# Half of a copy out of PSUM replaced by a sum that reads PSUM, in a four-layer graph network

## The chip, the cores and the metric

The kernel runs on one core of one Trainium2 chip. The metric is the time of the whole program on the device in microseconds (us), the median of three runs. The engines are named as in the profile: PE is TensorE (matmuls), PEld its weight loads, DVE is VectorE, ACT is ScalarE, POOL is GpSimd, SP is SyncE, which issues all the transfers here.

## The reference, cut to what matters

Sixty-four graphs of 256 nodes with 128 features each pass through four layers, every one closed by a residual and a layer norm. All of them multiply the node features by 256 x 256 matrices that are the same for all graphs:

```python
# layer 0: five gated steps, both matrices are adj
m  = einsum('nm,bmd->bnd', adj, h)
u3 = h @ u3_w.T + u3_b
z  = sigmoid(concat([m, m]) @ w3_w.T + w3_b + u3)
r  = sigmoid(concat([m, m]) @ w4_w.T + w4_b + u3)
hv = tanh(concat([m, m]) @ w5_w.T + w5_b + (r * h @ u5_w.T + u5_b))
h  = (1 - z) * h + z * hv
# layer 1: softmax over masked edges, split into its diagonal and the rest
# layer 2: attention over the edges, then relu(LN(.)), then (1 + eps) * g + adj @ g, two dense layers
# layer 3: adj @ x, adj @ adj @ x, adj @ adj @ adj @ x, each with its own weights
```

The product of a 256 x 256 matrix with the features of two graphs is what the change touches. It is needed eight times for each pair of graphs: five times in layer 0 and once in each of the others.

## The kernel before, in words

The graphs are worked on in 32 pairs, so that one tile is 128 partitions by 512 columns: two graphs, two blocks of 128 nodes each, 128 features. All data are float32. Many pairs are under way at once, and the order in which each engine meets their operations is worked out before the program is written. The class `Schedule` collects every operation with its readers and writers, its engine or a choice of engines, and an estimated duration. `Schedule.order` then repeatedly takes the operation that can start first by its own estimates, gives it the engine on which it would end first, and emits it. `SPARE` (L49) is a bias in that choice: microseconds added to the end an engine would reach, so that a positive number makes the engine less attractive. Its key `"DVE+"` stands for DVE operations that read two SBUF tensors[...] (`USES`, L45). At run time each engine follows its list strictly in order and waits on semaphores.

The helper `spread7` (L553) computes the product with a 256 x 256 matrix by 7 block products of 128 x 128 in place of 8. Its steps, all in one PSUM bank `t` of 512 columns (four blocks):

- three sums of the input blocks (L572, L573, L574), each on DVE or POOL;
- a first group of four block products (L576 to L579, all issued from L566), one into each block of `t`;
- a copy of all four blocks from `t` to the SBUF tile `o` (L580; the helper `evacuate` issues it from L236 on ACT, or from L237 on DVE);
- a sum of 256 columns (L581): blocks 0 and 1 of `o` plus blocks 2 and 3 of `o`, on DVE or POOL;
- a second group of three products (L582 to L584) that accumulate onto blocks 0, 3 and 1 of `t`. Each of them writes the bank that the copy reads, so none starts before the copy has ended;
- a sum of 128 columns (L585, DVE or POOL), a copy of block 0 (L586, again issued from L236) and a last sum of 256 columns that reads `t` (L587, DVE). Its result is the mT or qT that the following matmuls read.

A case of it is used 234 times: in all five steps of layer 0 from the third pair on (150), and in the other three layers for all but the last four pairs (84). The rest goes through `spread` (L542) with 8 block products.

Around it: L684, L685, L692, L699 and L700 are the 512-column matmuls of layer 0; L688, L694 and L703 its three tanh on ACT; L704, L705 and L707 its updates on DVE. L529 is a blockwise transpose on DVE ahead of a transfer out (L531) and back (L537), which turns a tile. L721 are the products of layers 1 and 2, L791 those of the attention, L827, L828 and L835 those of layer 3. L645 and L653 belong to the row scales, L617 and L622 are two ways (DVE, ACT) of a normalization.

Of the kernel before, what the change touches and what calls it, by code (L numbers as in the profile page):

```python
# [12 lines left out]
P = 128  # L13
# [32 lines left out]

AGAIN = {"DVE": 0.12, "POOL": 0.12}

SPARE = {"DVE": 1.0, "DVE+": 0.0, "POOL": -0.3}  # L49


DUE, LAST_DUE, LAST = 15.0, 12.0, 12
# [6 lines left out]
def mm(cols):  # L59

    return cols * 0.00168 + 0.005
# [40 lines left out]
class Schedule:  # L102
# [29 lines left out]
    def order(self, tiles):  # L132
# [14 lines left out]
        while ready:  # L147
            best = None
            for op in ready:
# [7 lines left out]
                for engine, us, fn in op.ways:  # L157
                    us = us if engine == "PE" else us * MARGIN
                    start = max(op.ready, held, *(engines[e] for e in USES.get(engine, (engine,))))
                    end = start + us + SPARE.get(engine, 0.0)  # L160
                    if way is None or end < way[0]:
# [41 lines left out]
def kernel(ctx: ExitStack, tc: tile.TileContext, x, xT, adj, adjT, mats, cols, rows, out):  # L203
    nc = tc.nc
# [10 lines left out]
    def pe(us, fn, r, w):  # L215
        S.add([("PE", us, fn)], r, w)
# [4 lines left out]
    def dve(us, fn, r, w):  # L221
        S.add([("DVE", us, fn)], r, w)
# [11 lines left out]
    def evacuate(o, i, r, w, us=(0.49, 0.61)):  # L234

        S.add([("ACT", us[0], lambda: nc.scalar.copy(o(), i())),  # L236
               ("DVE", us[1], lambda: nc.vector.tensor_copy(o(), i()))], r, w)  # L237
# [242 lines left out]
    def bank():  # L480

        t = Value("PS", name="ps")
        t.full = True
        return t
# [68 lines left out]
    def spread7(h, right, terms):  # L553

        sv, o, t = Value("A", name="sums"), Value("A", name="mT"), bank()
        p1, p2, p4 = (Part(sv) for _ in range(3))
        blk = lambda v, k: v.at(512)[:, k * P:(k + 1) * P]
        H = lambda b, j: lambda: blk(h, 2 * b + j)  # L560
        B = lambda j, i: lambda: right.ap[:, j, i * P:(i + 1) * P]
        T = lambda k: lambda: terms.ap[:, k, :]
        s3, s1, s2, s4 = (lambda k=k: blk(sv, k) for k in range(4))

        def product(k, left, rt, r, start=False):
            pe(mm(128), lambda: nc.tensor.matmul(blk(t, k), left(), rt(), start=start, stop=True, skip_group_check=True),  # L566
               [*r, right, terms, *[t] * (not start)], [t])

        def sum_(us, us_pool, fn, r, w):
            S.add([("DVE+", us, lambda: fn(nc.vector)), ("POOL", us_pool, lambda: fn(nc.gpsimd))], r, w)  # L570

        sum_(0.335, 0.8, lambda e: e.tensor_sub(sv.at(4, P)[:, 0:2], h.at(4, P)[:, 0::2], h.at(4, P)[:, 2:4]), [h], [p1])  # L572
        sum_(0.2, 0.46, lambda e: e.tensor_sub(s2(), s1(), H(0, 0)()), [h, p1], [p2])  # L573
        sum_(0.2, 0.46, lambda e: e.tensor_add(s4(), s2(), H(0, 1)()), [h, p2], [p4])  # L574

        product(0, H(0, 0), B(0, 0), [h], start=True)  # L576
        product(1, s1, T(0), [p1])
        product(3, s3, T(2), [p1])
        product(2, s2, T(1), [p2])  # L579
        evacuate(lambda: o.at(512), lambda: t.at(512), [t], [o])  # L580
        sum_(0.335, 0.8, lambda e: e.tensor_add(sv.at(4, P)[:, 0:2], o.at(4, P)[:, 0:2], o.at(4, P)[:, 2:4]), [o], [p1])  # L581
        product(0, H(0, 1), B(1, 0), [h])  # L582
        product(3, H(1, 1), T(3), [h])
        product(1, s4, B(1, 1), [p4])  # L584
        sum_(0.2, 0.46, lambda e: e.tensor_add(blk(o, 3), blk(sv, 0), blk(sv, 1)), [p1], [o])  # L585
        evacuate(lambda: blk(o, 0), lambda: blk(t, 0), [t], [o], (0.17, 0.2))  # L586
        dve(0.335, lambda: nc.vector.tensor_add(o.at(4, P)[:, 1:3], t.at(4, P)[:, 1::2],  # L587
                                                blk(sv, 0)[:, None, :].to_broadcast([P, 2, P])), [t, p1], [o])
        return o
# [87 lines left out]
    def layer0(x0, hT):  # L677
        h = x0
        for s in range(STEPS):
            mT = spread7(h, aT, aT7) if s in FAST and FIRST <= S.pair < n_pairs - FINAL else to_sbuf(spread(h, aT), "mT")  # L680
            t = bank()

# [43 lines left out]
    def layer1(x1):  # L726
        qT = spread7(x1, offT, offT7) if S.pair < n_pairs - SEVEN["q1"] else to_sbuf(spread(x1, offT), "qT")
        xb = Value("A", name="xb")
        xd = Value("A", name="xd")
        dc = lambda: dcol.ap[:, None, :, None].to_broadcast([P, 2, 2, D])  # L730

        def scaled():
            for c in range(4):
                nc.scalar.mul(tokens(xd)[:, c, :], tokens(x1)[:, c, :], dcol.ap[:, c % 2:c % 2 + 1])
        S.add([("ACT", 1.26, scaled), ("DVE+", TT, lambda: nc.vector.tensor_mul(xd.at(2, 2, D), x1.at(2, 2, D), dc())),
               ("POOL", 1.27, lambda: nc.gpsimd.tensor_mul(xd.at(2, 2, D), x1.at(2, 2, D), dc()))], [x1, dcol], [xd])
        dT = turn(xd, "dT", "x1")
        dve_or_pool(lambda e: e.tensor_add(tokens(xb), tokens(x1), row("l1_bias", 4)), [x1, rbc], [xb])
        t = seed((0.49, 0.61), tokens, lambda: tokens(xb), [xb, qT, dT])
        scale_norm(products([qT, dT], [lambda: mat("l1w1"), lambda: mat("l1w0")], t), x1)  # L740

    def layer2(x2):
# [44 lines left out]
        for b in range(2):  # L787
            def fn(b=b, t=t):
# [11 lines left out]
               ("DVE+", 0.34, lambda: nc.vector.tensor_scalar(hg.at(512), hg.at(512), 0.0, None, op0=ALU.max))], [hg], [hg])  # L800
        dve_or_pool(lambda e: e.tensor_add(tokens(hb), tokens(hg), row("b2", 4)), [hg, rbc], [hb])
        gT = spread7(hg, ginT, ginT7) if S.pair < n_pairs - SEVEN["g"] else to_sbuf(spread(hg, ginT), "gT")
        t, z = seed((0.49, 0.61), tokens, lambda: row("b1", 4), [rbc, gT]), Value("A", name="z")
        scale_norm(products([gT], [lambda: mat("w1")], t), z)
# [97 lines left out]
```

## Time and profile before

| | before |
|---|---|
| device time, median of 3 (lowest to highest) | 1486.76 us (1484.88 to 1487.45) |
| profiled span, first to last instruction | 1485.2 us |
| PE busy | 1474.5 us, 99% |
| DVE busy | 1234.4 us, 83% |
| ACT busy | 1026.9 us, 69% |
| POOL busy | 829.8 us, 56% |
| mean granted TensorE clock | 0.999 |

A busy share says how much of the span an engine had an instruction running. For PE it needs care: matmuls overlap, and their ends are modelled, so that the share alone does not say whether the array is fed without gaps. A group of instructions in the profile is written as line, engine, operation, output<-inputs, shapes, count, then busy time and mean duration of one in ns, then the idle time of the engine ahead of them and what ended it. Each float32 matmul of the program leaves two records in the trace.

### The profile page before, as it was taken

The numbers are of one execution on the slowest core, as the hardware profiler recorded it, in microseconds if no ns is written. First come the engines' busy times: TensorE is split into PE (matmuls) and PEld (weight loads), VectorE is DVE, ScalarE is ACT, GpSimd is POOL, SyncE is SP. The second block draws the span as 40 slices with busy tenths as digits, with TensorE's granted clock in tenths as the row PEclk, the third lists the DMA queues.
The fourth block names the chain that finished last, engine by engine and source line by source line (L and its number), as shares of the span: only waits on it lengthen the run. The fifth ranks groups of instructions, "written<-read, shape, count | busy, mean of one in ns | idle before, by whom it ended". The sixth has DMA issues, their size and how long they took to land.

```text
span 1485.2 us, 28119 instructions
## 1 busy us (share of the span) xinstructions
PE 1474.5 (99%) x7704; PEld 1062.6 (72%) x7704; DVE 1234.4 (83%) x3083; ACT 1026.9 (69%) x3116; POOL 829.8 (56%) x1307
## 2 busy tenths in 40 slices
PE   9999999999999999999999999999999999999998
PEld 6556666666676677777767777777676776788997
DVE  7767888988999899888888888878888888989872
ACT  3444556667777787876776767676686767878875
POOL 4412434555576776564556556565454746676542
PEclk9999999999999999999999999999999999999999
DMA  8544565777788978776778668777777776667762
GB/s 239 121 85 99 104 131 121 144 148 152 156 156 173 176 167 171 161 160 135 148 148 178 134 134 174 155 158 143 142 166 148 151 153 124 136 136 148 165 123 71
DMA packets 946845, 216.60 MB, mean 146 GB/s; under 512 B 726017, under 2 KB 942209, under 8 KB 946689
## 3 DMA queue, kind: packets, MB, share of 16 engines
q1 hardware_dynamic: 946688, 214.81, 70.7%
q8 instruction: 62, 1.02, 0.3%
q14 instruction: 95, 0.77, 0.2%
HBM read 116.86 MB, written 97.85 MB: 145 GB/s over the span
## 4 chain that ended last, share of the span: by engine, by line
PE 95%; DVE 2%; DMA 1%; ACT 0%; issue 0%; SPq 0%; POOL 0%; POOLq 0%; ACTq 0%; DVEq 0%
PE ps L566 23%; PE ps L699 9%; PE ps L700 9%; PE ps L684 9%; PE ps L685 9%; PE ps L692 9%; PE ps L721 7%; PE ps L835 4%; PE ps L828 4%; PE ps L827 4%; PE ps L791 4%; PE ps L548 2%; PE ps L751 2%; DMA x<-x_in 1%; DMA a<-e 0%; DVE a L529 0%
## 5 line engine op out<-in xcount | busy, mean ns | idle before, releaser
L566 PEld LDWEIGHTS ps<-aT,a 128*128 128x128 f32 x2144 | 291.4, 192 | 83.3 <-issue 76.7
L236 ACT COPY a<-ps 128x128 f32<-128x128 f32 (+2 forms) x553 | 230.4, 433 | 137.8 <-PE ps L566 48.6
L566 PE MATMUL ps<-aT,a 128*128 128x128 f32 x2144 | 315.7, 275 | 0.9 <-DMA a<-e 0.5
L585 POOL TENSOR_TENSOR a<-a 128x128 f32<-128x128 f32 x205 | 103.7, 510 | 150.4 <-DVE a L581 110.6
L688 ACT ACTIVATE a<-ps,bzrh 128x512 f32<-128x512 f32 x160 | 110.0, 688 | 104.4 <-PE ps L685 90.7
L703 ACT ACTIVATE ps<-ps,bzrh 128x512 f32<-128x512 f32 x160 | 106.1, 663 | 105.3 <-PE ps L700 102.3
L699 PE MATMUL ps<-a,w 128*128 128x512 f32 x320 | 163.7, 593 | 0.0
L685 PE MATMUL ps<-a,w 128*128 128x512 f32 x320 | 163.4, 592 | 0.0
L700 PE MATMUL ps<-a,u5h 128*128 128x512 f32 x320 | 163.4, 592 | 0.0
L692 PE MATMUL ps<-a,w 128*128 128x512 f32 x320 | 162.8, 593 | 0.0
L645 ACT ACTIVATE a<-ps 128x128 f32<-128x128 f32 x488 | 128.7, 282 | 45.9 <-PE ps L721 20.9
L529 DVE STREAM_TRANSPOSE a<-a 128x512 f32<-128x512 f32 x215 | 149.7, 700 | 10.9 <-DMA e<-a 2.2
L587 DVE TENSOR_TENSOR a<-ps,a 128x256 f32<-128x256 f32 x234 | 96.5, 416 | 67.8 <-ACT a L236 32.0
L721 PE MATMUL ps<-W,a 128*128 128x128 f32 x1024 | 144.5, 275 | 0.0
L721 PEld LDWEIGHTS ps<-W,a 128*128 128x128 f32 x1024 | 132.8, 192 | 16.1 <-issue 13.9
L653 POOL TENSOR_TENSOR s<-s,neg_half 128x4 f32<-128x4 f32 x128 | 138.1, 1079 | 7.6
L694 ACT ACTIVATE a<-ps,bzrh 128x512 f32<-128x512 f32 x160 | 110.5, 691 | 45.2 <-PE ps L692 37.8
L684 PE MATMUL ps<-a,W 128*128 128x512 f32 x256 | 131.0, 593 | 0.0
L685 PEld LDWEIGHTS ps<-a,w 128*128 128x128 f32 x320 | 60.8, 190 | 76.5 <-issue 68.1
L700 PEld LDWEIGHTS ps<-a,u5h 128*128 128x128 f32 x320 | 60.8, 190 | 76.5 <-issue 64.8
L705 DVE SCALAR_TENSOR_TENSOR ps<-a,ps 128x512 f32<-128x512 f32 x160 | 109.7, 686 | 6.1 <-ACT a L694 4.4
L573 POOL TENSOR_TENSOR a<-a,a 128x128 f32<-128x128 f32 x133 | 67.3, 507 | 83.6 <-DVE a L572 55.3
(208 smaller groups left out, 3329.2 us busy)
## 6 DMA issues: line engine op xcount, KB each, us to landing
e<-a SPq DMA_DIRECT2D x277, 256.0 KB
a<-e SPq DMA_DIRECT2D x1108, 64.0 KB
e<-b SPq DMA_DIRECT2D x32, 512.0 KB
b<-e SPq DMA_DIRECT2D x128, 128.0 KB
x<-x_in SPq DMA_DIRECT2D x32, 256.0 KB
t<-xT_in SPq DMA_DIRECT2D x32, 256.0 KB
a<-d SPq DMA_DIRECT2D x32, 256.0 KB
y_out<-a SPq DMA_DIRECT2D x32, 256.0 KB
```

What stands on the lines that cost most here:

```text
L236: S.add([("ACT", us[0], lambda: nc.scalar.copy(o(), i())), ("DVE", us[1], lambda: nc.vector.tensor_copy(o(), i()))], r, w)
L529: dve(n / 512 * 0.55 + 0.09, lambda: nc.vector.transpose(st.at(n), i.at(n)), [i], [st])
L566: pe(mm(128), lambda: nc.tensor.matmul(blk(t, k), left(), rt(), start=start, stop=True, skip_group_check=True), [*r, right, terms, *[t] * ...
L645: nc.scalar.activation(tokens(junk)[:, c, :], v.at(len(tiles), D)[:, k, :], AF.Square, scale=D ** -0.5, accum_out=mv()[:, c, 1:2])
L653: pool(1.02, lambda: nc.gpsimd.tensor_tensor(rs(), rs(), neg_half.ap, op=ALU.pow), [s, neg_half], [s])
L684: nc.tensor.matmul(t.at(512), mat("u3"), hT.at(512), start=True, stop=False)
L685: nc.tensor.matmul(t.at(512), w4.ap, mT.at(512), start=False, stop=True)
L692: pe(mm(512), lambda t=t, mT=mT: nc.tensor.matmul(t.at(512), w3.ap, mT.at(512), start=False, stop=True, skip_group_check=True), [w3, mT, t ...
L694: act(0.59, lambda t=t, z=z: nc.scalar.activation(z.at(512), t.at(512), AF.Tanh, bias=bzrh.ap[:, 0:1], scale=0.5), [t, bzrh], [z])
L699: nc.tensor.matmul(t.at(512), w5.ap, mT.at(512), start=True, stop=False)
L700: nc.tensor.matmul(t.at(512), u5h.ap, r.at(512), start=False, stop=True)
L721: nc.tensor.matmul(tokens(t)[:, c, :], tokens(i)[:, c, :], w(), start=(first and k == c == 0), stop=(k == len(lefts) - 1), skip_group_chec ...
```

## The change

Only blocks 2 and 3 of the first group are still copied to `o`. The sum of L581 takes its blocks 0 and 1 straight from the PSUM bank, and blocks 2 and 3 from the copy. POOL is no longer a choice for it: it is a DVE operation. The estimate given for the copy is halved, from (0.49, 0.61) to (0.29, 0.335) us for ACT and DVE. Since the sum now reads `t`, the second group of products waits for it as well as for the copy. In the bias table, DVE operations with two SBUF inputs get 0.2 us where they had 0.0. The purpose is less copying on ACT, no slow 256-column sum on POOL, and a division of the remaining sums between DVE and POOL that suits it.

```diff
-SPARE = {"DVE": 1.0, "DVE+": 0.0, "POOL": -0.3}
+SPARE = {"DVE": 1.0, "DVE+": 0.2, "POOL": -0.3}
...
         product(2, s2, T(1), [p2])
-        evacuate(lambda: o.at(512), lambda: t.at(512), [t], [o])
-        sum_(0.335, 0.8, lambda e: e.tensor_add(sv.at(4, P)[:, 0:2], o.at(4, P)[:, 0:2], o.at(4, P)[:, 2:4]), [o], [p1])
+        evacuate(lambda: o.at(512)[:, 2 * P:], lambda: t.at(512)[:, 2 * P:], [t], [o], (0.29, 0.335))
+        dve(0.335, lambda: nc.vector.tensor_add(sv.at(4, P)[:, 0:2], t.at(4, P)[:, 0:2], o.at(4, P)[:, 2:4]), [t, o], [p1])
         product(0, H(0, 1), B(1, 0), [h])
```

The order of the whole program is worked out anew from these estimates, so that nearly every engine's list is rearranged from the first pairs on. The matmuls are the same 3880 in both programs.

## Prediction

> **What bounds the kernel now.** I read the busy shares first, then the stretches of time, then what PE waited for, then a piece of PE's timeline, and last the end of the chain. The page's first line:
>
> ```profile
> PE 1474.5 (99%) x7704; PEld 1062.6 (72%) x7704; DVE 1234.4 (83%) x3083; ACT 1026.9 (69%) x3116; POOL 829.8 (56%) x1307
> ```
>
> PE is named, but a modelled busy share proves little. So I check it by counting. In PE's timeline (start, duration, operation, count) the starts give what one matmul takes when the next is ready:
>
> ```profile
> 704.63 1.02 PE L700 MATMUL ps<-a,u5h 128*128 128x512 f32 x2
> 705.48 0.83 PE L566 MATMUL ps<-aT,a 128*128 128x128 f32 x6
> 706.15 0.39 PE L566 MATMUL ps<-ginT,a 128*128 128x128 f32 x2
> ```
>
> Two records of 512 columns (one matmul) take 705.48 - 704.63 = 0.85 us, six of 128 columns (three matmuls) 706.15 - 705.48 = 0.67, so 0.223 each. Longer runs give 0.858 and 0.2225 us, and 0.431 for 256 columns. The program's instruction list holds 800 matmuls of 512 columns, 488 of 256, 128 of 130 and 2458 of 128: 686.4 + 210.4 + 28.8 + 546.9 = 1473 us (six narrow ones add 0.6). Until the first data matmul that is not held up, at 6.83 us, 3.4 us are not such slots (a start and warm-up matmuls at a low rate); after the last matmul, 1479.25, come 5.95 us to the end. Together 1473.1 + 3.4 + 5.9 = 1482.4 of a span of 1485.2. So PE lost only about 3 us. The stretches say where (length, then busy us of PE, PEld, DVE, ACT and POOL):
>
> ```profile
> 200.00:400.00 200.00, 200.00 (x991) 132.58 (x990) 173.80 (x394) 133.70 (x365) 103.09 (x160) 1.00 0.71 143
> 400.00:600.00 200.00, 197.94 (x1088) 143.31 (x1087) 184.22 (x462) 154.21 (x478) 143.34 (x220) 1.00 0.84 167
> 600.00:800.00 200.00, 200.00 (x1081) 145.56 (x1080) 166.97 (x430) 146.09 (x461) 115.62 (x184) 1.00 0.75 155
> 1200.00:1400.00 200.00, 199.01 (x1188) 159.48 (x1188) 179.30 (x507) 155.96 (x531) 129.65 (x194) 1.00 0.72 146
> 1460.00:1486.00 26.00, 18.93 (x86) 15.69 (x84) 4.39 (x17) 10.12 (x42) 5.04 (x9) 0.94 0.25 61
> ```
>
> 2.06 us are missing at 400 to 600, where DVE is busiest (92%), 0.99 at 1200 to 1400, the rest at both ends. What PE waited for, in total, times, longest (the first line of the answer, a start-up wait, is left out):
>
> ```profile
> PE ps L751 <- DVE a L810: 0.9, 1, 0.9
> PE ps L566 <- ACT a L236: 0.7, 1, 0.7
> PE ps L566 <- DMA a<-e: 0.5, 1, 0.5
> PE ps L566 <- DMA x<-x_in: 0.5, 1, 0.5
> PE ps L566 <- DVE a L572: 0.4, 1, 0.4
> PE ps L828 <- ACT a L236: 0.3, 1, 0.3
> ```
>
> Only one or two single waits are on the copies that the change touches, 0.7 + 0.3 us. The rows of these operations (out<-in, count | busy, mean ns | idle before, what ended it):
>
> ```profile
> L236 ACT COPY a<-ps 128x512 f32<-128x512 f32 x262 | 151.9, 590 | 61.3 <-PE ps L566 27.7 <-PE ps L548 19.1 <-DMA d<-a 2.0
> L236 ACT COPY a<-ps 128x256 f32<-128x256 f32 x59 | 22.2, 376 | 31.6 <-PE ps L828 31.0 <-issue 0.2
> L587 DVE TENSOR_TENSOR a<-ps,a 128x256 f32<-128x256 f32 x234 | 96.5, 416 | 67.8 <-ACT a L236 32.0 <-PE ps L566 31.8 <-POOL s L608 1.2
> L581 POOL TENSOR_TENSOR a<-a 128x256 f32<-128x256 f32 x99 | 73.6, 746 | 70.2 <-ACT a L236 65.2 <-DMA a<-e 4.7
> L581 DVE TENSOR_TENSOR a<-a 128x256 f32<-128x256 f32 x135 | 58.3, 436 | 14.6 <-ACT a L236 10.7 <-DMA a<-e 1.9 <-issue 0.9
> ```
>
> [...] a 512-column record lasts 593 ns while the next starts after 429; hence the count above. [...] L581 on DVE, two SBUF inputs, ran 376 to 953 ns; L587, one input in PSUM, 377 to 426. The new sum is of the second kind. [...] The trace doesn't show that for this sum (medians 418 and 424 ns), so I use 416. [...]
>
> **The change part by part.** Counts are those of the two programs' instruction lists, durations those of the rows.
>
> Copies. On ACT, 230 copies of 512 columns become 228 of 256: 230 x 0.590 = 135.7 to 228 x 0.376 = 85.7, so -50 us of ACT. POOL's and DVE's other work moves some to ACT: L622 +28 x 0.436, L645 +16 x 0.476, L734 +20 x 0.32, L799 +2 x 0.63, L665 -14 x 0.30, together +23. ACT: about -27, to 1000.
>
> Sums. POOL loses 99 x 0.746 = 74 us. DVE gains 99 x 0.416 = 41 and saves 135 x 0.02 = 3 on those it had.
>
> Bias. With 0.2 us against it, DVE gives away input sums (33 of L572, 33 of 128 columns: 25 us), 28 of L617 (10), 16 statistics pairs (7) and 22 operations of 512 columns (19), and gains 7 of L667 (+3); smaller ones give -1. DVE: +41 - 3 - 61 + 3 - 1 = about -21, to 1213. POOL gets 33 x 0.78 + 33 x 0.51 + 20 x 1.37 = 70 back and ends at -4. PE: the same 3880 matmuls, 0.
>
> All of this lies beside PE, which hides it: a saving on ACT, DVE or POOL shortens nothing while PE has work.
>
> The chain. Before, the second group waits for a 0.59 us copy; after, for 0.376 + 0.416 us and a second hand-over (0.05 to 0.25, estimated from the pauses of 0.04 to 0.25 us between dependent engines in the timeline): +0.25 to +0.45 us, 234 times. Behind the waiting sum stand DVE's other operations (L704, L705, L707, L529). Would PE notice? I measured in PE's lists, in the slots above, how much other PE work stands between the end of the first group and the start of the second. Shortest tenth, median, longest tenth begin at 1.8, 3.0 and 7.0 us before and at 2.8, 4.5 and 10.2 after: 1.0 to 1.5 us more at the short end and middle, for 0.45 more needed. From the last product to the first reader of mT it is 2.8 and 4.2 before, 2.6 and 4.1 after, with the same operations between. So the new order has paid for its longer chain, on paper, with work of other pairs. A bank is held longer, median of first to last product 8.3 to 9.8 us, with eight banks; I cost that at 0 to 5 us and take 0, as PE's list is equally dense.
>
> The end. Before, PE waits about 0.7 us at 1473 for the copy of the last L548 result. In the new list 1.7 us of L835 stand between these two; I take -0.5.
>
> Sum: PE's 1473 unchanged, start unchanged, end -0.5, about 3 us of gaps of the old order replaced by as many of the new one. 1486.76 - 0.5 = 1486.3.
>
> **The rivals.** A, faster: DVE is less full, above all at 400 to 600, and the gaps vanish. That takes away 2.06 + 0.99 and 0.5 at the end: 1486.8 - 3.5 = 1483.3, and little below it is possible, since no matmul goes. For it: the gaps stand where DVE is fullest. Against: the reshuffle can make others. B, slower by the longer chain: if the tenth with least distance is late after queueing on ACT and then DVE, 23 cases x 0.3 us = 7 us: 1494. For it: the sum on DVE already waited up to 2.5 us for the copy, and PE gives no slack back. Against: the longer distances. C, slower by reordering: a new order meets two or three unlucky transfers of the kind seen at 400 to 600 (1 to 2 us each), or fuller queues in a stretch: +5, 1492. Nothing in the profile excludes it; DMA is at 0.84 there.
>
> **How the numbers follow.** No change (within 0.2%, 3 us) 0.43; A 0.17; B 0.23; C 0.17. Some of B and C would be quite long, since losses have no limit and gains end near 1483. Chances: faster 0.17, same 0.43, slower 0.40. The range runs from just under A, 1482, past B to 1499, where some 20 cases lose 0.6 us each; it leaves out 0.04 below and 0.14 above.
>
> **What would show it.** Right: PE busy about 1474 of the span with gaps of 2 to 5 us, ACT near 1000, DVE near 1213, POOL near 826; L581 near 416 ns with a narrow spread; hardly any PE wait on L581. Wrong toward B: many PE waits on DVE L581. Wrong toward C: stretches of PE under 198 of 200 that end on transfers or other DVE work. Wrong toward A: every inner stretch at 200.0. If matmul slots themselves differ, my floor is wrong.

## The result and the profile after

| | before | after |
|---|---|---|
| device time, median of four runs (lowest to highest) | 1487.1 us (1484.9 to 1487.6) | 1498.6 us (1497.5 to 1499.4) |
| ratio to before, 95% interval | | 1.008 (1.0062 to 1.0097) |
| profiled span | 1485.2 us | 1496.3 us |

The change costs 0.8%. The first line of the page of after shows that the three engines it was to relieve are relieved:

```profile
PE 1479.5 (99%) x7704; PEld 1064.5 (71%) x7704; DVE 1214.9 (81%) x3038; ACT 998.7 (67%) x3182; POOL 803.6 (54%) x1294
```

DVE lost 20 us, ACT 28, POOL 26, and the program still became 11 us longer. PE does the same 3880 matmuls and is busy for 5 us more: its work is stretched, and its idle time grew from 10.7 to 16.8 us. The rows of the changed operations, from the groups of after with shapes kept apart, and the spread of the sum (minimum, median, maximum in ns) from its line:

```profile
L236 ACT COPY a<-ps 128x256 f32<-128x256 f32 x287 | 105.1, 375 | 74.7 <-PE ps L566 33.2 <-PE ps L828 27.1 <-DMA e<-a 3.4
L581 DVE TENSOR_TENSOR a<-ps,a 128x256 f32<-128x256 f32 x234 | 93.7, 408 | 12.4 <-ACT a L236 11.8
```

```profile
L581 DVE TENSOR_TENSOR a<-ps,a x234: 372/414/425, 16.8 to 1434.0; 128x256 f32<-128x256 f32 x117
```

Copy and sum do what they were meant to: 375 ns and 408 ns, and no sum over 425 ns. What PE waited for in after, longest first (waited for, us in total, times, longest; the list goes on with shorter ones):

```profile
PE ps L548 <- DVE a L800: 3.2, 1, 3.2
PE ps L548 <- DVE a L667: 1.5, 1, 1.5
PE ps L566 <- DMA a<-e: 1.4, 2, 1.2
PE ps L296 <- DVE ones L294: 1.2, 1, 1.2
PE ps L566 <- DVE a L581: 0.9, 2, 0.6
PE ps L566 <- ACT a L694: 0.8, 1, 0.8
```

Only 0.9 us is on the changed sum. The long waits are on L800 and L667, lines that the change doesn't touch, and both fall into the last 100 us.

To see all of the loss I took from each trace, for each two matmul records that follow one another, the time between their starts less the slot of the first (0.111 us for 128 columns or fewer, 0.1125 for 130, 0.2156 for 256, 0.429 for 512), and added up what was over 0.05 us. This lost time holds PE's waits and slow stretches alike; 2.3 us of it in before and 2.9 in after fall in the first 10 us, where the first eight matmul records (L296) alone take 3.5 and 3.6 us.

| lost on PE, us | whole | 400 to 800 | 1340 to 1440 | rest |
|---|---|---|---|---|
| before | 9.0 | 3.6 | 1.9 | 3.5 |
| after | 20.1 | 7.2 | 8.5 | 4.5 |

The difference, 11.1 us, is the whole difference of the spans. It stands at two places: at 400 to 800, where all layers are in the works, and in the drain, where the last pairs end. Of the 3.6 us at 400 to 800, only 1.0 came before 600, where DVE is fullest (busy 176.66 of 200 us in after); the rest came at 600 to 800. The largest single piece is at 1415 us. From after's DVE timeline (start, duration, operation; "..." stands for rows left out):

```profile
1412.84 0.42 DVE L766 CUSTOM_DVE_ANT_0 b<-a,maskb 128x256 f32<-128x256 f32 x1 [0.50 <-DMA a<-d]
...
1413.54 1.49 DVE L766 CUSTOM_DVE_ANT_0 b<-a,maskb 128x256 f32<-128x256 f32 x1
...
1415.90 0.69 DVE L810 SCALAR_TENSOR_TENSOR a<-ps,x 128x512 f32<-128x512 f32 x1
1416.63 0.87 DVE L600 BATCH_NORM_STATS2 s<-a 128x6 f32<-128x128 f32 x4
1417.42 0.36 DVE L602 BATCH_NORM_AGGREGATE s<-s 128x2 f32<-128x6 f32 x4
1417.70 0.66 DVE L798 TENSOR_TENSOR a<-a,rbc 128x512 f32<-128x512 f32 x1
1418.39 0.43 DVE L800 TENSOR_SCALAR a<-a 128x512 f32<-128x512 f32 x1
```

And PE at the same time:

```profile
1415.09 0.59 PE L828 MATMUL ps<-vq,a 128*128 128x256 f32 x2
1418.87 2.63 PE L548 MATMUL ps<-ginT,a 128*128 128x256 f32 x8 [3.18 <-DVE a L800]
1421.29 2.98 PE L835 MATMUL ps<-a,a2T 128*128 128x256 f32 x8
```

PE has nothing to do until L800 of one of the last pairs is done. L800 stands on DVE behind the L766 of another pair, which had waited for a transfer, and behind the layer norm of a third. In before, L548 on ginT follows L828 at 1414.11 with PE at work throughout:

```profile
1413.68 0.59 PE L828 MATMUL ps<-vq,a 128*128 128x256 f32 x2
1414.11 1.89 PE L548 MATMUL ps<-ginT,a 128*128 128x256 f32 x8
1415.84 1.95 PE L791 MATMUL ps<-h,b 128*128 128x128 f32 x16
```

So this loss is a matter of which pair's work stands where, not of the sum's own duration. Whether the change caused that order or merely drew it was the question for the runs.

### The profile page after: what moved, and what is told of

The parts are those of the page before. It is cut to its first block, busy times and chain, and to the rows that moved or that the text cites. A ratio compares the mean times of both kernels' runs of the same rounds, so it can differ in the third digit from the quotient of the medians.

```text
span 1496.3 us, 28025 instructions
## 1 busy us (share of the span) xinstructions
PE 1479.5 (99%) x7704; PEld 1064.5 (71%) x7704; DVE 1214.9 (81%) x3038; ACT 998.7 (67%) x3182; POOL 803.6 (54%) x1294
## 5 line engine op out<-in xcount | busy, mean ns | idle before, releaser
L236 ACT COPY a<-ps 128x256 f32<-128x256 f32 (+2 forms) x551 | 179.1, 344 | 143.9 <-PE ps L566 57.2
L587 DVE TENSOR_TENSOR a<-ps,a 128x256 f32<-128x256 f32 x234 | 96.3, 417 | 85.5 <-ACT a L236 47.8
L645 ACT ACTIVATE a<-ps 128x128 f32<-128x128 f32 x504 | 133.3, 284 | 48.2 <-PE ps L721 29.3
L572 POOL TENSOR_TENSOR a<-a 128x256 f32<-128x256 f32 x94 | 70.7, 752 | 112.9 <-DMA a<-e 32.9
```

The costliest lines, as they stand in the source:

```text
L236: S.add([("ACT", us[0], lambda: nc.scalar.copy(o(), i())), ("DVE", us[1], lambda: nc.vector.tensor_copy(o(), i()))], r, w)
L645: nc.scalar.activation(tokens(junk)[:, c, :], v.at(len(tiles), D)[:, k, :], AF.Square, scale=D ** -0.5, accum_out=mv()[:, c, 1:2])
```

## The experiments

Theories: **chain** (the hand-over from copy to sum to second group is late at run time), **bias** (0.2 against two-input DVE operations is harmful), **POOL** (DVE gets sums that POOL took), **order** (the plan made under the new dependency is worse), and **luck** (any new order is worse than the one of before). Each ratio is to runs of before on the same chip; those had medians of 1486.6 to 1487.9 us.

**One part alone.** The first run has only the bias:

```diff
-SPARE = {"DVE": 1.0, "DVE+": 0.0, "POOL": -0.3}
+SPARE = {"DVE": 1.0, "DVE+": 0.2, "POOL": -0.3}
```

> The kernel before with only the bias of two-input DVE operations raised from 0.0 to 0.2; copy and sum stay as they were. If the bias is what costs (it gives the whole program another order and moves input sums to POOL): 1494 to 1500 us, with PE gaps of 10 us or more. If the sum out of PSUM costs: 1485 to 1489 us. If any new order costs a random few us: somewhere from 1485 to 1500, which this run alone cannot tell.

Measured: 1494.5 us, ratio 1.0047 (1.0032 to 1.0062). Lost on PE: 15.8 us, 8.5 of it in the drain.

The second is the kernel after with `"DVE+": 0.0`.

> The kernel after with the bias back at 0.0: half copy and sum out of PSUM stay. If the sum out of PSUM and its longer chain cost: 1495 to 1501 us. If the bias costs: 1485 to 1489 us. If the two only cost together or any new order costs a random amount: in between.

Measured: 1503.9 us, 1.011 (1.0093 to 1.0126), lost 26.5 us, 14.5 of it at 400 to 600. The parts don't add: +7.1 for the bias, +16.5 for the sum, but +11.5 for both. In these orders the bias made the change's plan better, and the old one worse.

The third takes POOL away from the sum:

```diff
-        sum_(0.335, 0.8, lambda e: e.tensor_add(sv.at(4, P)[:, 0:2], o.at(4, P)[:, 0:2], o.at(4, P)[:, 2:4]), [o], [p1])
+        dve2(0.335, lambda: nc.vector.tensor_add(sv.at(4, P)[:, 0:2], o.at(4, P)[:, 0:2], o.at(4, P)[:, 2:4]), [o], [p1])
```

> The kernel before, with POOL no longer a choice for the 256-column sum; it stays a sum of two SBUF inputs behind a full copy. If losing POOL as a way out for 99 sums is what costs: 1494 to 1500 us. If reading PSUM (second group waits for the sum) is what costs: 1485 to 1489 us.

Measured: 1491.2 us, 1.0026 (1.0015 to 1.0036). That lies between the two readings. Losing POOL can be a part; in this draw (one order that the planner makes) it is 3.8 us.

**Order or operations.** The next run keeps the order of after on every engine and puts the old operations into it:

```diff
-        evacuate(lambda: o.at(512)[:, 2 * P:], lambda: t.at(512)[:, 2 * P:], [t], [o], (0.29, 0.335))
-        dve(0.335, lambda: nc.vector.tensor_add(sv.at(4, P)[:, 0:2], t.at(4, P)[:, 0:2], o.at(4, P)[:, 2:4]), [t, o], [p1])
+        evacuate(lambda: o.at(512), lambda: t.at(512), [t], [o], (0.29, 0.335))
+        dve(0.335, lambda: nc.vector.tensor_add(sv.at(4, P)[:, 0:2], o.at(4, P)[:, 0:2], o.at(4, P)[:, 2:4]), [t, o], [p1])
```

> Every engine's order is exactly that of the kernel after, but the operations are the old ones: the copy takes all four blocks (0.59 us in place of 0.376) and the sum reads two SBUF inputs, so that the second group of products waits only for the copy. If the order itself holds the gaps (mainly the drain of the last pairs, at 1390 to 1425 us): 1495 to 1502 us, the stall near 1415 us still there. If the hand-over from ACT to DVE inside the chain makes the gaps: at or below 1491 us.

Measured: 1502.1 us, 1.0098 (1.0083 to 1.0113), lost 21.8 us. Its PE waits begin like those of after:

```profile
PE ps L548 <- DVE a L800: 3.1, 1, 3.1
PE ps L566 <- DMA a<-e: 2.1, 1, 2.1
PE ps L548 <- DVE a L667: 1.4, 1, 1.4
```

The same two waits of the drain, with no sum out of PSUM in the program. Here the second group needn't wait for the sum at all, so the hand-over is not what makes them.

The converse keeps the order of before, and puts the new operations in wherever that order has the sum on DVE and ahead of the second group (`engine` and `start` are what the plan gave each operation):

```diff
-        evacuate(lambda: o.at(512), lambda: t.at(512), [t], [o])
-        sum_(0.335, 0.8, lambda e: e.tensor_add(sv.at(4, P)[:, 0:2], o.at(4, P)[:, 0:2], o.at(4, P)[:, 2:4]), [o], [p1])
+        n_copy = len(S.ops)
+        direct = lambda: S.ops[n_copy + 1].engine == "DVE+" and (S.ops[n_copy + 1].start, n_copy + 1) < min(
+            (S.ops[n_copy + k].start, n_copy + k) for k in (2, 3, 4))
+        first = lambda: 2 * P if direct() else 0
+        evacuate(lambda: o.at(512)[:, first():], lambda: t.at(512)[:, first():], [t], [o])
+        sum_(0.335, 0.8, lambda e: e.tensor_add(sv.at(4, P)[:, 0:2], (t if direct() else o).at(4, P)[:, 0:2], o.at(4, P)[:, 2:4]), [o], [p1])
```

> Every engine's order is exactly that of the kernel before, but wherever that order has the sum on DVE and ahead of the second group (86 of 234 cases), the sum reads blocks 0 and 1 from PSUM and the copy takes two blocks only; the other 148 stay as they were. If the operations themselves are harmless and only the order counts: 1485 to 1489 us, gaps of PE within 2 us of the 9 of before. If the longer chain from ACT to DVE to PE costs: at least 86/234 of the 11 us, so 1491 us or more, with PE waits on the sum.

Measured: 1486.9 us, 0.9997 (0.9989 to 1.0006). Its sums (the lines are shifted by six; L587 is the sum here):

```profile
L587 DVE TENSOR_TENSOR a<-ps,a 128x256 f32<-128x256 f32 x86 | 35.1, 412 | 10.3 <-ACT a L238 8.3 <-DMA a<-e 1.7
L587 DVE TENSOR_TENSOR a<-a 128x256 f32<-128x256 f32 x49 | 21.1, 433 | 0.7 <-POOL a L591 0.6
```

So 86 sums out of PSUM cost nothing that can be measured under the old order, against 4.2 us (86/234 of 11.5) if the chain itself cost. These 86 are cases in which the old order already had the sum in time, so this run alone says nothing of the other 148. The run before it covers all 234: in the order of after, taking the chain away gains nothing, if with longer copies. With both, chain falls as the main cause: the loss lies in the order.

**Luck.** Two runs nudge the planner under the old operations. The first has `TT = 0.615` in place of 0.61:

> The kernel before, same operations, with one estimate of the planner moved by under 1% (a 512-column DVE operation, 0.61 to 0.615). If almost any new order is worse than the one of before, which was a lucky or a searched one: 1490 to 1500 us, with the gaps in other places and the drain (1340 to 1440 us) worse. If orders are about equally good and the change's own order is bad for a reason of its own: 1485 to 1489 us.

Measured: 1488.8 us, 1.0004 (0.9996 to 1.0013), though most of PE's list is rearranged. The second has `MARGIN = 1.105` in place of 1.1:

> The kernel before, same operations, with the planner's margin on all durations but PE's moved from 1.1 to 1.105. Same two readings as for the run with the moved 512-column estimate: 1490 to 1500 us if any new order costs, 1485 to 1489 us if orders are equally good.

Measured: 1486.3 us, 0.999 (0.9983 to 0.9997). Orders rearranged throughout can be as good as that of before. Two runs nudge the kernel after, one with a bias of 0.1, one with the same margin of 1.105:

> The kernel after with the bias at 0.1, between its 0.2 (1498.6) and the 0.0 of the run with the sum alone (1503.9). If the bias acts smoothly: about 1501 us. If it acts only by drawing another order: anywhere from 1487 to 1506 us, not between the two.

Measured: 1497.8 us, 1.0066 (1.0046 to 1.0085).

> The kernel after with the planner's margin moved from 1.1 to 1.105, the nudge that left the kernel before at 0.999 of its time. If the change's orders are worse in general: 1494 to 1504 us. If the kernel after merely drew a bad order: 1485 to 1492 us.

Measured: 1493.3 us, 1.0044 (1.003 to 1.0059). Four orders drawn with the change (1493.3, 1497.8, 1498.6, 1503.9) are all slower than the three drawn close to before (1486.3, 1487.1, 1488.8). Luck explains the scatter among the four; the step between the groups it leaves unexplained. But the nudges of the old plan moved an estimate by under 1%, and larger moves with the old operations cost too: 1491.2 us with POOL taken from the sum, 1494.5 with the bias alone. So a further reading stays open: that the plan of before sits at a good spot, and that most larger moves away from it lose some us.

**What in the plan.** The planner is told that the sum reads the bank; nothing else is changed, so on the chip copy and sum are the old ones, POOL included:

```diff
-        sum_(0.335, 0.8, lambda e: e.tensor_add(sv.at(4, P)[:, 0:2], o.at(4, P)[:, 0:2], o.at(4, P)[:, 2:4]), [o], [p1])
+        sum_(0.335, 0.8, lambda e: e.tensor_add(sv.at(4, P)[:, 0:2], o.at(4, P)[:, 0:2], o.at(4, P)[:, 2:4]), [t, o], [p1])
```

> The kernel before with one thing of the change alone: the planner is told that the 256-column sum also reads the PSUM bank, so that the second group is planned behind it. Copy of four blocks, sum of two SBUF inputs, POOL as a choice and bias 0.0 stay. If the longer chain in the plan is what makes the new orders worse (a bank is held longer, the second group comes later): 1494 us or more, with PE gaps over 15 us. If the forced DVE sum or the bias is: 1485 to 1490 us.

Measured: 1496.2 us, 1.0067 (1.0048 to 1.0087), lost 17.9 us. This dependency alone, with no new operation on the chip, costs 9.6 us in its draw, of the size of the 11.5. It does two things in the plan: the product's result comes later, and its bank is held longer. The longer hold is there on the chip as well. From the first product of a 7-product multiplication to the end of its L587 (instances told apart by the order of each engine's list), the median of the 234 is 10.0 us in before, 11.6 in after, 12.2 with the dependency alone, but 10.0 with the bias alone, which cost its 7.1 us without a longer hold. To see whether banks matter at all, the kernel before was planned with `"PS": (512, 7)` in place of 8:

> The kernel before, planned with 7 PSUM banks in place of 8. If the banks bind the order (so that holding one longer costs, as the change does): 1495 us or more, gaps of PE in the same stretches (400 to 600 and 1340 to 1440 us). If there are banks to spare: 1485 to 1490 us.

Measured: 1493.5 us, 1.0046 (1.0031 to 1.0061). One bank of eight fewer cost 6.9 us in this draw, less than was expected if banks bind, and not where after loses most: in the drain it lost 1.8 us, before 1.9. Then each effect by itself, in the planner only. Later result (1.2, then 1.6 us after L587), the bank free as before:

```diff
-                x.ready = max(x.ready, end + (AGAIN.get(engine.rstrip("+-"), 0.0) if same else op.seen))
+                x.ready = max(x.ready, end + getattr(op, 'late', 0.0) + (AGAIN.get(engine.rstrip("+-"), 0.0) if same else op.seen))
...
+        last.late = 1.2
```

> The kernel before, all operations as they were; only the planner is told that the result of each 7-product multiplication is usable 1.2 us later (the PSUM bank is not counted as held longer). If the later result of each of the eight multiplications of a pair is what worsens the orders: 1493 us or more, as with the dependency alone (1496.2). If the longer held bank is: 1485 to 1490 us.

Measured: 1493.2 us, 1.0045 (1.003 to 1.006).

> The same with 1.6 us, a second draw of an order under the same condition, since single orders scatter by a few us. Later result as the cause: 1493 us or more. Held bank as the cause: 1485 to 1490 us.

Measured: 1486.9 us, 1.0001 (0.9993 to 1.001). Bank held longer (1.2, then 1.6 us), the result usable as before:

```diff
-                        free[v.cls].append((v.end, v.ap))
+                        free[v.cls].append((v.end + getattr(v, 'extra', 0.0), v.ap))
...
+        t.extra = 1.2
```

> The kernel before, all operations as they were; only the planner is told that the bank of each 7-product multiplication comes free 1.2 us later (the result is usable as before). If the held bank is what worsens the orders: 1493 us or more. If the later result is: 1485 to 1490 us. Both slower: each has a part.

Measured: 1500.0 us, 1.0085 (1.007 to 1.01), lost 22.4 us.

> The same with the bank held 1.6 us longer, the second draw. Held bank as the cause: 1493 us or more. Later result as the cause: 1485 to 1490 us.

Measured: 1497.4 us, 1.0076 (1.006 to 1.0093), lost 17.1 us. The stretches 400 to 600 and 1340 to 1440 us follow (length, then busy us of PE, PEld, DVE, ACT, POOL; last the PE clock, the DMA share and GB/s). Before had 197.94 us of PE in the first, and in the second:

```profile
1340.00:1440.00 100.00, 99.01 (x637) 89.91 (x636) 87.10 (x285) 84.14 (x329) 61.19 (x87) 1.00 0.77 153
```

With the result 1.2 us late, then 1.6 us late:

```profile
400.00:600.00 200.00, 195.90 (x1064) 140.12 (x1064) 180.19 (x453) 146.57 (x465) 134.56 (x210) 1.00 0.80 158
1340.00:1440.00 100.00, 97.98 (x638) 88.25 (x637) 85.93 (x268) 85.69 (x331) 61.38 (x87) 1.00 0.77 151
```

```profile
400.00:600.00 200.00, 198.41 (x1083) 143.25 (x1082) 180.57 (x457) 151.11 (x475) 140.74 (x222) 1.00 0.83 163
1340.00:1440.00 100.00, 99.26 (x640) 90.00 (x639) 85.85 (x287) 84.05 (x339) 63.68 (x93) 1.00 0.79 153
```

With the bank held 1.2 us longer:

```profile
400.00:600.00 200.00, 195.82 (x1043) 139.67 (x1042) 176.43 (x440) 148.97 (x467) 135.38 (x209) 0.98 0.77 155
1340.00:1440.00 100.00, 95.65 (x632) 86.33 (x631) 84.35 (x269) 84.85 (x338) 64.67 (x93) 1.00 0.79 153
```

After:

```profile
400.00:600.00 200.00, 197.35 (x1086) 142.90 (x1085) 176.66 (x465) 153.24 (x503) 142.68 (x219) 1.00 0.84 167
1340.00:1440.00 100.00, 94.74 (x622) 85.61 (x621) 82.94 (x256) 85.38 (x340) 58.96 (x90) 0.98 0.77 153
```

PE's busy us are what to read. At 400 to 600 they don't tell the two effects apart: 195.90 with the result 1.2 us late, 195.82 with the bank held 1.2 us longer. In the drain the held bank comes closer to after. The lost time says the same:

| lost on PE, us | whole | 400 to 800 | 1340 to 1440 |
|---|---|---|---|
| after | 20.1 | 7.2 | 8.5 |
| result late by 1.2, by 1.6 | 15.2, 9.1 | 7.6, 2.5 | 3.6, 1.9 |
| bank held longer by 1.2, by 1.6 | 22.4, 17.1 | 9.7, 5.8 | 6.2, 6.6 |
| dependency alone | 17.9 | 5.3 | 4.8 |
| bias alone | 15.8 | 2.2 | 8.5 |

Both draws with a held bank cost over 10 us; of the two with a late result one cost 6.4 and one nothing. Planning the bank as held longer is thus enough for a loss of this size. That it is what makes after's loss is likely but not shown: a part of the later result isn't excluded, and the bias alone opens as large a gap in the drain with neither.

**A better version?** The kernel before with a margin of 1.05, which packs the plan tighter:

> The kernel before with the planner's margin at 1.05, a candidate for a version better than both. Less margin packs the plan tighter. If what the plan then promises holds on the chip: 1480 to 1485 us, near the floor of 1483. If the margin covers real delays: PE waits appear, 1488 us or more.

Measured: 1496.8 us, 1.0069 (1.0054 to 1.0084). It lost 6.8 us at 400 to 800 and 6.4 in the drain. So an order of the old operations can be nearly as bad as that of after, with no dependency added, once the estimates are moved far enough. No run was better than before by more than 0.1%; that one is the margin of 1.105.

## Why the prediction was wrong

It forecast no change at 1486.3 us; the time was 1498.6, just below the upper end of its range, 1499. That is luck: the range went so far for some 20 late hand-overs of 0.6 us each, which did not happen.

- **PE is the bound, and only gaps can be won or lost**: right. The slots of all records add up to about 1466 us in both traces, and the longer span is lost time on PE alone. The forecast's own sum, 1473, was some 7 us too high. It gave every matmul two records, but the 52 transposes (44 of L523, 8 of L376) and four bfloat16 products (L365) left one each. So before had not 3 us of gaps to lose or win but 6.7 (9.0 less 2.3 in the first 10 us), and the floor of rival A, 1483, was too high.
- **Loads**: DVE about 1213 us, measured 1214.9; ACT about 1000, measured 998.7; POOL near 826, measured 803.6. All three fell, and nothing followed from it. POOL's operations moved in the forecast numbers (33 of L572, 33 of 128 columns, 20 of 512), but each took less time than in before (L572 785 to 767 ns, L574 508 to 493, L782 1370 to 1285), so POOL got back 53 us and not 70. In both traces a L572 on POOL that overlapped a DVE operation with all its inputs in SBUF (a TENSOR_TENSOR or L766) took longer, 883 ns in the mean before and 871 after, than one that didn't (745 and 747), and fewer overlapped in after: 26 of 158, against 36 of 125. That is the way L572 moved; no run tests it by itself.
- **The sum at 416 ns with a narrow spread**: right, 408 ns, 372 to 425; the median was 414, and 418 for the old sum on DVE, so no extra cost of a PSUM source shows.
- **The end, -0.5 us**: right. Beyond 1440 us the lost time fell from 0.8 to 0.3 us.
- **The chain, +0.25 to +0.45 us, covered by other pairs' work**: right as far as it goes. PE waited 0.9 us for L581 in all, and the same order with the old operations is no faster. Rival B, slower by late hand-overs, is not what happened.
- **The step that failed** is the next one: "A bank is held longer, median of first to last product 8.3 to 9.8 us, with eight banks; I cost that at 0 to 5 us and take 0, as PE's list is equally dense." With it fell the term of the sum that rests on it, "about 3 us of gaps of the old order replaced by as many of the new one": the lost time went from 9.0 to 20.1 us. A list without times shows no gaps: it holds the same matmuls whatever they wait for. The plan has times, and its own length, which `Schedule.order` leaves in `span`, had grown from 1487.9 to 1491.8 us. What the runs show in its place: the new order by itself, with the old operations in it, costs 14.7 us (1502.1), and planning the banks as held 1.2 or 1.6 us longer costs 13.2 and 10.6, the dependency alone 9.6, one bank fewer 6.9. That the bank is the main reason for after's order stays likely, not shown. (The plan's length is no safe guide either: it is 1491.9 with the result 1.6 us late, which lost nothing, and 1482.6 with the margin of 1.05, which lost 10.2.)
- **Rival C, slower by reordering**, had the direction, and at +5 us half the size. Its reasons, unlucky transfers or fuller queues, name where single gaps end, not what makes the plan worse.

What stays open: the 9.6 us and the 11.5 us are each from one drawn order, and single orders scatter (1493.3 to 1503.9 with the change); so the parts of dependency, lost POOL and bias in the 11.5 us can't be told apart to a few us. Nor is it known how many larger moves of the old plan would lose as much: the three that told the planner of neither a later result nor a longer hold (no POOL for the sum, the bias, the margin of 1.05) all did lose: 3.8, 7.1 and 10.2 us.

## What to carry to other kernels

When the bounding engine is near its floor, unloading the others wins little, and an added dependency is judged by what it holds: here a sum moved to PSUM saved 28 us of ACT and held an accumulation bank about 1.6 us longer (medians 10.0 and 11.6), 234 times. Where a scheduler decides the order, separate operations from order: put the old operations in the new order, and the new ones in the old order, before blaming either. And nudge an irrelevant estimate a few times: without that scatter (here 2.5 us among the old plan and its two nudges, and 10.6 among the plans with the change) a single comparison of two plans says little.

## What the runs showed of the hardware beyond that

After the stall of 3.3 us at 1415 us PE ran at about half rate for a while. Two stretches of after; the number after the five engines is the granted clock:

```profile
1419.00:1424.00 5.00, 5.00 (x16) 4.10 (x17) 4.80 (x11) 2.98 (x10) 2.86 (x4) 0.66 1.05 161
1424.00:1430.00 6.00, 6.00 (x45) 5.72 (x44) 2.45 (x12) 4.75 (x21) 4.55 (x8) 1.00 0.85 188
```

Eight records of 256 columns started 0.39 to 0.43 us apart in place of 0.216, which added 1.6 us. Shorter stalls were followed by such a stretch too, but not every stall was. The run with the old operations in the new order stood still for 2.3 us at 545 us, and then had a granted clock of 0.55:

```profile
547.50:551.00 3.50, 3.50 (x11) 2.79 (x12) 3.40 (x7) 0.82 (x3) 2.19 (x5) 0.55 0.96 281
```

In all traces together there are 12 stalls of 2.0 to 3.4 us of lost time past the start. Seven were followed by a stretch at about half rate that cost 1.3 to 2.0 us more (the shortest of them was 2.01 us long, in the run with the bank held 1.2 us longer), five by none, the longest, 3.39 us in the run with the sum alone, among them (from 1422.47 to 1429.84 us, right behind that stall, its records of 256 columns started 0.216 us apart). So in these traces it is not the length of the stall alone that decides, and what decides is not shown.

Just ahead of the stall at 1415 us L766 (`tensor_tensor_reduce` in the kernel) took 1.49 us in place of 0.42, while POOL ran L797:

```profile
1413.40 1.34 POOL L797 TENSOR_TENSOR a<-a,rbc 128x512 f32<-128x512 f32 x1 [0.75 <-ACT a L665]
```

L766 started after L797 and ended 0.3 us after it. Both read two SBUF tensors. Of the 128 L766 of after, 16 took over 500 ns, and each of these overlapped a TENSOR_TENSOR on POOL; the 52 with nothing on POOL beside them took 380 to 426 ns. The changed sum, with one input in PSUM, never took over 425 ns. The old sum on DVE, with both inputs in SBUF, took over 500 ns in 9 of its 135 cases in before (up to 953), each time overlapping a TENSOR_TENSOR on POOL. So of these operations the slow ones read two SBUF tensors and ran beside POOL's, and here this struck one that the change left alone. As L800 stands behind it on DVE, about 1.1 us (an estimate, 1.49 less 0.42) of the longest gap comes from it.
